# A message-passing layer: node rows laid in pairs on a partition, and two skipped loops put inside one

## The chip, the cores and the metric

The kernel runs on one core of a Trainium2 chip. The metric is the time on the device in microseconds, lower is better. Before the change it is 2068.9 us, the median of 3 runs (2066.65 to 2071.43).

## What is computed

A graph layer over 6250 nodes with 128 features and 200,000 edges, sorted by destination. Cut to what matters, with `ssp(z) = softplus(z) - log 2`:

```python
h = jnp.maximum(layernorm(x), 0.0)
xw = h @ W_in                                       # [6250, 128]
W = ssp(edge_attr @ W_f1 + b_f1) @ W_f2 + b_f2      # [200000, 128], edge_attr has 20 columns
x_ij = xw[dst] * (W * edge_weight)
out = segment_sum(x_ij, src, num_segments=6250)
result = x + ssp(out @ W_o1 + b_o1) @ W_o2 + b_o2
```

The gather goes by `dst`, which is sorted, and the sum by `src`, which is random.

## The kernel before

The nodes are padded to 6272, that is 49 tiles of 128, and the edges to 784 chunks of 128. Four chunks (512 edges) are a quad; there are 391 quads, and one step of the main loop belongs to each. All of it is one function, `tile_gnn`, with many helpers. Up to line 1254 the order of the work on every engine is written out by hand (`tc.manual_schedule()`): the loop at line 1208 runs its fixed calls for step `i`, and between them the hooks that `at(i, point, fn, ...)` has put there. SyncE (SP) issues nearly all DMAs, in program order on one queue; a DMA waits there until the one that used its semaphore eight DMAs earlier has landed.

**Nodes.** `groups` are pairs of node tiles (256 nodes; the last has one). For each, `xt_load` (L175 to 177) brings rows of `x` to `x_sb`, `prep_stat` to `prep_x3` (L181 to 255) make the layer norm, relu and the product with `W_in`, split in three bfloat16 parts, and `tab_write` (L257) writes them to a table `tab` in DRAM, three rows a node. Group 0 comes before the loop, the others at intervals of nine steps within it.

**Edges.** `load_sc` (L288) brings per 1024 edges the edge features, the relative destinations and, for each 256 edges, a window of 21 nodes of `tab`. PE makes the filter (L313, L494, L505) and picks the nodes' rows (L497), ACT scales (L510), DVE multiplies (L520). The sum by source goes two ways. Part of the quads are scattered by indirect DMAs that POOL issues (`scatter`, L579 to 583) and that add into four accumulators in DRAM, `accs[0]` to `accs[3]`, of [6400, 128] float32 each, with further rows behind them for a list. The others are sorted and summed on PE (L687, L781) and added into `accT` (L792), an SBUF tile of [128 features, 6272 nodes].

**Accumulator 0.** It takes no scatters after a certain point (`RET`). From then on `r0_load` (L1062) brings it in groups of 512 nodes (`tgroups`: 12 of four tiles, one of a single tile), `r0_tp` (L1068) transposes the tiles on PE, and `r0_add` (L1075) adds them into `accT`.

**The flags.** At the end of the loop a few operations (L1256 to 1270) find whether an edge fell outside its window, a slot was full, or a value was large. Two loops over register trip counts follow: `For_i(0, anew)` at L1273 zeroes the accumulators, and `For_i(0, trips)` at L1280 does all edges anew, chunk by chunk. With the given inputs both run no trip. In front of each, every engine loads the trip count (L1272, L1278), and going past a loop, each engine passes a chain of waits on the semaphores of all DMAs and engines.

**The tail** (L1349 to 1446) is also ordered by hand. For each group of 512 nodes `t_load` (L1353) brings three accumulators from DRAM, three loads of 256 KB; POOL adds two of them (`t_sum1`, L1359), POOL or DVE the third (`t_sum2`, L1364); PE transposes (`t_tp`, L1370), DVE adds `accT` (`t_cp`, L1376), PE multiplies by `W_o1` (`t_z`), ACT makes the softplus in three passes (`t_ln`), DVE completes it (`t_act`), PE multiplies by `W_o2` (`t_y`), and `t_out` (L1412) adds `x_sb` (with the bias already in it) and writes the result. Five groups are loaded ahead. At step `j` SP issues the loads of group `j + 5` first and then the output of group `j - 4`, so three outputs stand between the last loads:

```python
for j in range(-1, TG + 4):
    if TAIL_AHEAD <= j + TAIL_AHEAD < TG:
        for k in (1, 2, 3):
            t_load(j + TAIL_AHEAD, k)
    ...
    if 0 <= j - 4 < TG:
        t_out(j - 4)
```

In `x`, the accumulators, `accT` and the result, partition `p` of tile `t` holds node `128 t + p`: a partition's piece of one tile is one row of 128 float32, 512 bytes in one run in DRAM. In the table a piece is 768 bytes.

Of the kernel before, what the change touches and what calls it, by code (L numbers as in the profile page):

```python
# [20 lines left out]
P = 128  # L21
# [33 lines left out]
def tile_gnn(ctx: ExitStack, tc: tile.TileContext, x, fB, cT, srcT, srcr, dstr, win_, wf1, wf2, bias, bo1c, wo1,  # L55
# [780 lines left out]
    with tc.manual_schedule():  # L836
# [238 lines left out]
        def r0_add(g):  # L1075
            o, T = tgroups[g]
            v = accT[:, o:o + T * P]
            u = pst["p", g].rearrange("p t f -> p (t f)")[:, :T * P]
            nc.vector.tensor_tensor(v, u, v, op=ALU.add)
# [188 lines left out]
    flagi = cp.tile([1, 2], I32, name="flagi")  # L1268
# [3 lines left out]
    anew = nc.values_load(flagi[:, 1:2], min_val=0, max_val=1, skip_runtime_bounds_check_because="0 or 1")  # L1272
    with tc.For_i(0, anew, 1):  # L1273
        nc.vector.memset(accT, 0.0)
        for k in range(1, NACC):
            for j in range(ZR):
                zero_piece(nc.sync, k, j)
    trips = nc.values_load(flagi[:, 0:1], min_val=0, max_val=NCH,  # L1278
                           skip_runtime_bounds_check_because="0 or the number of chunks")
    with tc.For_i(0, trips, 1) as ci:  # L1280
        dcol = wk.tile([P, 1], I32, bufs=1, tag="dcol", name="dcol")
        nc.sync.dma_start(dcol, dstr.rearrange("s (e o) -> (s e) o", o=1)[bass.ds(ci * P, P), :])
        rcol = wk.tile([P, 1], BF16, bufs=1, tag="rcol", name="rcol")
        nc.sync.dma_start(rcol, reld.rearrange("s (e o) -> (s e) o", o=1)[bass.ds(ci * P, P), :])
        scol = wk.tile([P, 1], I32, bufs=1, tag="scol", name="scol")
        nc.sync.dma_start(scol, srcr.rearrange("s (e o) -> (s e) o", o=1)[bass.ds(ci * P, P), :])
        ccol = wk.tile([P, 1], F32, bufs=1, tag="ccol", name="ccol")
        nc.sync.dma_start(ccol, cT[:, bass.ds(ci, 1)])
        xcol = wk.tile([P, 1], BF16, bufs=1, tag="xcol", name="xcol")
        cm = wk.tile([1, 1], I32, bufs=1, tag="cm", name="cm")  # L1290
        nc.sync.dma_start(cm, cmap[0:1, bass.ds(ci, 1)])
        _, (cr,) = nc.values_load_multi_w_load_instructions(
            cm, engines=[SP], min_val=0, max_val=EP // P - 1,
            skip_runtime_bounds_check_because="a column of the table")
        nc.sync.dma_start(xcol, dropd[:, bass.ds(cr, 1)])
        sb = wk.tile([P, P], I32, bufs=1, tag="oeq", name="fsb")
        nc.sync.dma_start(sb, srcr.rearrange("s e -> (s e)")[bass.ds(ci * P, P)].unsqueeze(0).to_broadcast([P, P]))
        ft = wk.tile([P, P], BF16, tag="oh", name="fft")
        nc.vector.memset(ft[96:P, :], 1.0)
        fsel = fsd.rearrange("b g (r e) -> b (g r) e", r=RB)  # L1300
        for g, m in FPARTS:
            nc.sync.dma_start(ft[g * RB:(g + m) * RB, :], fsel[bass.ds(ci // (BE // P), 1), :m * RB,
                                                               bass.ds((ci % (BE // P)) * P, P)]
                              .rearrange("o m e -> (o m) e"))
        x3 = wk.tile([P, 3, P], BF16, tag="pt", name="fx3")
        nc.gpsimd.indirect_dma_start(out=x3.rearrange("p k f -> p (k f)"), out_offset=None,
                                     in_=tab.rearrange("(n k) f -> n (k f)", k=3),
                                     in_offset=bass.IndirectOffsetOnAxis(ap=dcol[:, 0:1], axis=0))
        ok = wk.tile([P, 4], F32, bufs=1, tag="ok", name="ok")
        nc.vector.tensor_scalar(ok[:, 0:1], rcol, float(WIN), None, op0=ALU.is_ge)  # L1310
        nc.vector.tensor_scalar(ok[:, 1:2], rcol, 0.0, None, op0=ALU.is_lt)
        nc.vector.tensor_tensor(ok[:, 2:3], ok[:, 0:1], ok[:, 1:2], op=ALU.add)
        nc.vector.tensor_tensor(ok[:, 2:3], ok[:, 2:3], zcol[:, 3:4], op=ALU.max)
        nc.vector.scalar_tensor_tensor(ok[:, 3:4], ok[:, 2:3], xcol, ccol, op0=ALU.max, op1=ALU.mult)
        xw = wk.tile([P, P], F32, bufs=1, tag="rm", name="fxw")
        nc.vector.tensor_tensor(xw, x3[:, 0], x3[:, 1], op=ALU.add)
        nc.vector.tensor_tensor(xw, xw, x3[:, 2], op=ALU.add)
        z = ps.tile([P, P], F32, tag="A", name="fz", bufs=4)
        nc.tensor.matmul(z, ws, ft[:K1, :], start=True, stop=True)
        e = wk.tile([P, P], F32, tag="a", name="fe")  # L1320
        nc.scalar.activation(e, z, AF.Abs)
        nc.scalar.activation(e, e, AF.Exp, scale=-1.0)
        nc.scalar.activation(e, e, AF.Ln, bias=half, scale=0.5)
        a = wk.tile([P, P], F32, tag="a", name="fa")
        nc.vector.scalar_tensor_tensor(a, z, 0.0, e, op0=ALU.max, op1=ALU.add)
        W = ps.tile([P, P], F32, tag="A", name="fW", bufs=4)
        nc.tensor.matmul(W, onesb[HB:], b2rep[HB:, 0, :], start=True, stop=False)
        nc.tensor.matmul(W, a, w2, start=False, stop=True)
        m = wk.tile([P, 132], F32, tag="xc", name="fm")
        nc.vector.tensor_copy(m[:, 128:129], wgt)  # L1330
        nc.vector.scalar_tensor_tensor(m[:, :P], W, ok[:, 3:4], xw, op0=ALU.mult, op1=ALU.mult)
        eq = wk.tile([P, P], F32, tag="eq", name="feq", bufs=3)
        nc.vector.tensor_tensor(eq, sb, scol.to_broadcast([P, P]), op=ALU.is_equal)
        pp = ps.tile([P, 132], F32, tag="B", name="fpp", bufs=4)
        nc.tensor.matmul(pp[:, :129], eq, m[:, :129], start=True, stop=True)
        s = wk.tile([P, P], F32, bufs=1, tag="dg", name="fs")
        nc.scalar.copy(s, pp[:, :P])
        dlt = wk.tile([P, 2], F32, bufs=1, tag="dlt", name="dlt")
        nc.vector.tensor_scalar(dlt[:, 0:1], scol, trash, None, op0=ALU.subtract)
# [256 lines left out]
```

## Time and profile before

| | |
|---|---|
| median of 3 runs | 2068.9 us (2066.65 to 2071.43) |
| the profiled execution | 2079.2 us, its span 2077.4 us |
| PE's mean granted clock | 0.963 |
| busy share of PE, DVE, ACT, POOL | 90%, 80%, 71%, 79% |
| DMA packets, bytes | 381188, 272.57 MB, mean 131 GB/s |

PE is TensorE's matrix products and PEld its weight loads, DVE is VectorE, ACT ScalarE, POOL GpSimd, SP SyncE; a q behind a name (SPq) is the engine's instruction queue, where waits, branches and DMA issues stand. A group of instructions is shown as line, engine, operation, result<-operands, count, then busy time, mean duration in ns, and the idle time ahead of it with what ended it. A row of the view by time has the start in us, the duration, the engine, the line and the count. A row of the view by stretches has the stretch, its length, the busy time and the instructions of PE, PEld, DVE, ACT and POOL, then PE's granted clock (1.00 is full), the mean busy share of the 16 DMA engines (above 1 where packets overlap), and the rate in GB/s. A row of the view of one source line has the durations (min/median/max, ns) and the first and last start.

### The profile page before, as it was taken

To read this page: it belongs to the slowest core of one execution; us is meant where nothing else is said; L and a number is where in the kernel's file an instruction comes from. 1 tells how busy PE (TensorE), PEld (TensorE's weight loads), DVE (VectorE), ACT (ScalarE), POOL (GpSimd) and SP (SyncE) were. 2 spreads that over 40 slices of the span, in tenths; PEclk is the share of its full clock that TensorE was granted. 3 is DMA by queue.
4 is the path that set the end of the run, shared out by engine and by line. 5 is a ranking of instruction groups with operands and counts; after the bars stand their busy time and mean duration, and the time that the engine had idled before them with its cause. 6 is when DMAs were issued, how large, how long until landed. Compare 5 with 4: busy or idle time off the path is not lost. (4 is left out here: it accounts for less than half of the span.)

```text
span 2077.4 us, 57578 instructions
## 1 busy us (share of the span) xinstructions
PE 1862.5 (90%) x20381; PEld 1288.0 (62%) x20381; DVE 1659.4 (80%) x4448; ACT 1482.8 (71%) x4083; POOL 1643.9 (79%) x1040
## 2 busy tenths in 40 slices
PE   3579988899999999999999999999999999999956
PEld 2456666566666666666666666666666666677734
DVE  3678887797888888988988978979889788787635
ACT  2468776777776777777678777777877777788714
POOL 3578787888877888887878878888888888888774
PEclk9679999999999999999999999999999999999977
DMA  7887766667766766766667666676676676667648
GB/s 238 227 210 147 125 118 120 121 112 130 130 118 114 126 127 119 139 123 123 120 120 130 120 119 118 118 124 117 120 134 108 124 121 111 110 119 131 130 48 239
DMA packets 381188, 272.57 MB, mean 131 GB/s; under 512 B 97727, under 2 KB 341354, under 8 KB 380898
## 3 DMA queue, kind: packets, MB, share of 16 engines
q0 software_dynamic: 143728, 71.30, 35.2%
q1 hardware_dynamic: 236882, 197.50, 34.1%
q8 instruction: 161, 2.64, 0.5%
q14 instruction: 129, 1.06, 0.2%
q10 hardware_dynamic: 288, 0.07, 0.0%
HBM read 154.45 MB, written 114.24 MB: 129 GB/s over the span
## 5 line engine op out<-in xcount | busy, mean ns | idle before, releaser
L582 POOL DMA_INDIRECT acc<-s,lji x768 | 1245.7, 1622 | 266.6 <-issue 180.3
L687 PE MATMUL pq<-pt,pm 128*128 128x387 bf16 x2688 | 533.0, 341 | 44.6 <-DVE pt L676 10.6
L510 ACT ACTIVATE xc<-xg,cb 128x128 f32<-128x128 f32 x1564 | 446.4, 371 | 135.7 <-PE xg L497 119.9
L505 PE MATMUL W<-w,a 128*128 128x128 f32 x3128 | 464.1, 292 | 0.1
L505 PEld LDWEIGHTS W<-w,a 128*128 128x128 f32 x3128 | 388.4, 195 | 42.3 <-issue 3.1
L687 PEld LDWEIGHTS <-pm 128*128 128x128 bf16 x2688 | 260.3, 99 | 233.4 <-issue 37.2
L693 ACT CAST mst<-pq 128x387 bf16<-128x387 f32 x672 | 302.2, 481 | 135.0 <-PE pq L687 96.5
L781 PE MATMUL un<-so,mst 32*128 32x392 bf16 x8064 | 374.5, 327 | 17.3 <-DVE pr L627 7.0
L781 PEld LDWEIGHTS <-mst 32*128 32x128 bf16 x8064 | 227.8, 93 | 157.1 <-issue 60.2
L323 ACT ACTIVATE a<-a,con 128x512 f32<-128x512 f32 x391 | 282.3, 722 | 12.7
L582 POOL DMA_INDIRECT acc<-s,ji x123 | 200.2, 1628 | 80.4 <-issue 26.4
L318 ACT ACTIVATE a<-z 128x512 f32<-128x512 f32 x391 | 238.3, 610 | 26.8 <-PE z L313 17.2
L676 DVE TENSOR_TENSOR pt<-pt 128x512 f32<-128x512 f32 x336 | 231.8, 690 | 5.8
L662 DVE TENSOR_SCALAR pm<-iot,pos 128x576 bf16<-128x576 f16 x672 | 221.8, 391 | 0.0
L792 DVE TENSOR_TENSOR accT<-un,accT 128x392 f32<-128x392 f32 x320 | 158.6, 558 | 73.7 <-PE un L781 37.5
L520 DVE TENSOR_TENSOR s<-W,xc 128x512 f32<-128x512 f32 x192 | 131.9, 687 | 85.9 <-ACT xc L510 52.0
L766 DVE TENSOR_SCALAR so<-iot,mst 128x392 bf16<-128x392 f16 x672 | 191.0, 344 | 6.7 <-PE un L781 6.7
L582 POOL DMA_INDIRECT acc<-os,oji x96 | 156.4, 1629 | 31.2 <-issue 18.0
L497 PE MATMUL xg<-wn,oh 63*128 63x128 bf16 x1564 | 157.3, 222 | 15.8 <-ACT xc L510 9.4
L313 PE MATMUL z<-ft,ws 123*128 123x512 bf16 x391 | 152.0, 389 | 15.7 <-DVE iotl L941 9.4
L494 PE MATMUL W<-b2rep,onesb 64*128 64x512 bf16 x391 | 153.9, 394 | 0.0
L520 DVE TENSOR_TENSOR pt<-W,xc 128x512 f32<-128x512 f32 x168 | 115.2, 686 | 47.9 <-ACT xc L510 29.5
(209 smaller groups left out, 2435.5 us busy)
## 6 DMA issues: line engine op xcount, KB each, us to landing
rb<-reld SPq DMA_DIRECT2D x391, 64.0 KB
fsd<-f SPq DMA_DIRECT2D x49, 480.0 KB
ft<-fsd SPq DMA_DIRECT2D x195, 120.0 KB
sb<-src SPq DMA_DIRECT2D x169, 128.0 KB
fb<-in_fB_dram SPq DMA_DIRECT2D x49, 320.0 KB
ft<-fsd SPq DMA_DIRECT2D x195, 80.0 KB
wn<-tab SPq DMA_DIRECT2D x782, 15.8 KB
acc<-s,lji POOLq DMA_INDIRECT x768
```

Of the source, the lines that this page charges most:

```text
L318: nc.scalar.activation(a, st[q]["z"], AF.Exp)
L323: nc.scalar.activation(a, a, AF.Ln, bias=half, scale=0.5)
L505: nc.tensor.matmul(W[:, c, :], st[q]["a"][:, c * P:(c + 1) * P], w2, start=False, stop=(c == 3))
L510: nc.scalar.mul(xc[:, c, :], st[q]["xg"][:, c, :], late["c", q // CQ][:, 4 * (q % CQ) + c:4 * (q % CQ) + c + 1])
L520: nc.vector.tensor_tensor(m[:, :, :P], st[q]["W"], st[q]["xc"], op=ALU.mult)
L582: nc.gpsimd.indirect_dma_start(out=accs[k][:rows, :], out_offset=bass.IndirectOffsetOnAxis(ap=ji, axis=0), in_=s, in_offset=None, compute_ ...
L662: nc.vector.tensor_scalar(pm[:, c], iot[:, :SLOTS], rk[r]["pos"][:, 4 * j + c:4 * j + c + 1], None, op0=ALU.is_equal)
L676: nc.vector.tensor_tensor(pt[:, :, k * P:(k + 1) * P], a, high(a), op=ALU.subtract)
L687: nc.tensor.matmul(t[:, :PW], mp[q]["pm"][:, c, s * P:(s + 1) * P], high(mp[q]["pt"][:, c:c + 1, :PW])[:, 0], start=(c == 0), stop=(c == 3))
L693: nc.scalar.copy(mp[q]["ms", s][:, :PW], mp[q].pop(("q", s))[:, :PW])
L766: nc.vector.tensor_scalar(so, iotw[:, :GN], w[:, 3 * P // 2:3 * P // 2 + 1], None, op0=ALU.is_equal)
L781: nc.tensor.matmul(ts[g][:, :GN], mp[q]["ms", s][v, k * P:(k + 1) * P], mp[q]["oh"][v], start=(q == qs[0] and k == 0), stop=(q == qs[-1] a ...
```

## The change

Two things are changed.

The first is the layout of nodes. Within 256 nodes, partition `p` holds nodes `2p` and `2p + 1` in its two tiles, in place of `p` and `p + 128`. Four helpers say so: `rows` for a DRAM tensor, `wide` for a row-major SBUF tile, `nodes` for columns of `accT`, `tiles` for a transposed tile. The loads of `x`, of accumulator 0 and of the tail's three accumulators and the writes of the result then move runs of 1024 bytes, the table's writes runs of 1536. `accT` keeps its columns in the order of the nodes, so `r0_add` and `t_cp` reach it at every second column. Single tiles (the last of each grouping) stay as they were.

The second is the flags: `flagi` gets a third element, 0 or 1, and the two loops with the loads of their trip counts stand inside an outer loop over it. The bodies are the same, moved in by four columns.

On the engines, nothing changes its place up to the flags. Behind them DVE has one operation more, and every engine has one more loop head and loop end, of which the walk past it runs; the two inner ones are inside the part that is passed. GpSimd's wait and increment for the indirect DMAs (before, at the second loop) now stand at the outer loop too.

```diff
+    def rows(t, o, T):
+        n = min(T, 2)
+        return t[o:o + T * P, :].rearrange("(h p t) f -> p h (t f)", p=P, t=n)
+
+    def wide(t, T):
+        return t.rearrange("p (h t) f -> p h (t f)", t=min(T, 2))
+
+    def nodes(t, o, T):
+        return t[:, o:o + T * P].rearrange("f (h p t) -> f h t p", p=P, t=min(T, 2))
+
+    def tiles(t, T):
+        return t[:, :T].rearrange("f (h t) p -> f h t p", t=min(T, 2))
+
     def xt_load(g):
         o, T = groups[g]
-        nc.sync.dma_start(x_sb[:, o // P:o // P + T], x[o:o + T * P, :].rearrange("(t p) f -> p t f", p=P))
+        nc.sync.dma_start(wide(x_sb[:, o // P:o // P + T], T), rows(x, o, T))
...
     def tab_write(g):
         o, T = groups[g]
-        nc.sync.dma_start(tab[o * 3:(o + T * P) * 3, :].rearrange("(t p k) f -> p t k f", t=T, k=3),
+        nc.sync.dma_start(tab[o * 3:(o + T * P) * 3, :].rearrange("(p t k) f -> p t k f", t=T, k=3),
                           pst[g]["x3"][:, :T])
...
         def r0_load(g):
-            nc.sync.dma_start(t_[:, :T], accs[0][o:o + T * P, :].rearrange("(t p) f -> p t f", p=P))
+            nc.sync.dma_start(wide(t_[:, :T], T), rows(accs[0], o, T))
...
         def r0_add(g):
             o, T = tgroups[g]
-            v = accT[:, o:o + T * P]
-            u = pst["p", g].rearrange("p t f -> p (t f)")[:, :T * P]
-            nc.vector.tensor_tensor(v, u, v, op=ALU.add)
+            v = nodes(accT, o, T)
+            nc.vector.tensor_tensor(v, tiles(pst["p", g], T), v, op=ALU.add)
...
-    flagi = cp.tile([1, 2], I32, name="flagi")
+    flagi = cp.tile([1, 3], I32, name="flagi")
+    nc.vector.tensor_scalar(flagi[:, 2:3], flag1, 0.0, None, op0=ALU.is_gt)
...
-    anew = nc.values_load(flagi[:, 1:2], min_val=0, max_val=1, skip_runtime_bounds_check_because="0 or 1")
-    with tc.For_i(0, anew, 1):
...
-    trips = nc.values_load(flagi[:, 0:1], min_val=0, max_val=NCH,
-                           skip_runtime_bounds_check_because="0 or the number of chunks")
-    with tc.For_i(0, trips, 1) as ci:
...
+    redo = nc.values_load(flagi[:, 2:3], min_val=0, max_val=1, skip_runtime_bounds_check_because="0 or 1")
+    with tc.For_i(0, redo, 1):
+        anew = nc.values_load(flagi[:, 1:2], min_val=0, max_val=1, skip_runtime_bounds_check_because="0 or 1")
+        with tc.For_i(0, anew, 1):
...
+        trips = nc.values_load(flagi[:, 0:1], min_val=0, max_val=NCH,
+                               skip_runtime_bounds_check_because="0 or the number of chunks")
+        with tc.For_i(0, trips, 1) as ci:
...
         def t_load(g, k):
-            nc.sync.dma_start(t_[:, :T], accs[k][o:o + T * P, :].rearrange("(t p) f -> p t f", p=P))
+            nc.sync.dma_start(wide(t_[:, :T], T), rows(accs[k], o, T))
...
         def t_cp(g):
-            o, w = tgroups[g][0], tgroups[g][1] * P
-            oT = tk.tile([P, 512], F32, tag="oT", name="oT")
-            nc.vector.tensor_tensor(oT[:, :w], tl[g]["tp"].rearrange("p t f -> p (t f)")[:, :w], accT[:, o:o + w],
-                                    op=ALU.add)
-            tl[g]["oT"] = oT
+            o, T = tgroups[g]
+            oT = tk.tile([P, 4, P], F32, tag="oT", name="oT")
+            nc.vector.tensor_tensor(tiles(oT, T), tiles(tl[g]["tp"], T), nodes(accT, o, T), op=ALU.add)
+            tl[g]["oT"] = oT.rearrange("p t f -> p (t f)")
...
-            full = min(T, max(0, (N - o) // P))
-            if full:
-                nc.sync.dma_start(out[o:o + full * P, :].rearrange("(t p) f -> p t f", p=P), y[:, :full])
-            rest = min(N - o, w) - full * P
-            if rest > 0:
-                nc.sync.dma_start(out[o + full * P:o + full * P + rest, :], y[:rest, full, :])
+            if N - o >= w:
+                nc.sync.dma_start(rows(out, o, T), wide(y[:, :T], T))
+            else:
...
```

More of the change, by code (lines that the diff above doesn't have):

```diff
@@ L1273, in tile_gnn @@
[L1273 to L1278, printed above, removed]
-                           skip_runtime_bounds_check_because="0 or the number of chunks")
[L1280 to L1339, printed above, removed]
-        nc.vector.scalar_tensor_tensor(dlt[:, 1:2], pp[:, 128:129], wgt2, dlt[:, 0:1], op0=ALU.is_lt, op1=ALU.mult)
-        ji = wk.tile([P, 1], I32, bufs=1, tag="fji", name="fji")
-        nc.vector.tensor_scalar(ji, dlt[:, 1:2], trash, None, op0=ALU.add)
-        nc.gpsimd.indirect_dma_start(out=accs[1][:, :], out_offset=bass.IndirectOffsetOnAxis(ap=ji[:, 0:1], axis=0),
-                                     in_=s, in_offset=None, compute_op=ALU.add)
@@ L1416, in t_out @@
             nc.vector.tensor_tensor(y[:, :T], tl[g]["y"][:, :T], x_sb[:, o // P:o // P + T, :], op=ALU.add)
-            full = min(T, max(0, (N - o) // P))
-            if full:
-                nc.sync.dma_start(out[o:o + full * P, :].rearrange("(t p) f -> p t f", p=P), y[:, :full])
-            rest = min(N - o, w) - full * P
-            if rest > 0:
-                nc.sync.dma_start(out[o + full * P:o + full * P + rest, :], y[:rest, full, :])
+            if N - o >= w:
+                nc.sync.dma_start(rows(out, o, T), wide(y[:, :T], T))
+            else:
+                n = min(T, 2)
+                for h in range(T // n):
+                    b = o + h * n * P
+                    full, rest = divmod(min(max(N - b, 0), n * P), n)
+                    if full:
+                        nc.sync.dma_start(out[b:b + full * n, :].rearrange("(p t) f -> p t f", t=n),
+                                          y[:full, h * n:(h + 1) * n])
+                    if rest:
+                        nc.sync.dma_start(out[b + full * n:b + full * n + rest, :].rearrange("(p t) f -> p t f", p=1),
+                                          y[full:full + 1, h * n:h * n + rest])
             del tl[g]
```

68 lines of the change are left out of this document (added).

## Prediction

> **What bounds the kernel now.** The page's first section was read first, then the busy times by stretches of the span, then the order of time on POOL and on SP's queue near the end.
>
> ```profile
> span 2077.4 us, 57578 instructions
> PE 1862.5 (90%) x20381; PEld 1288.0 (62%) x20381; DVE 1659.4 (80%) x4448; ACT 1482.8 (71%) x4083; POOL 1643.9 (79%) x1040
> ```
>
> ```profile
> 31.00:40.00 9.00, 4.56 (x21) 3.80 (x22) 4.50 (x6) 1.32 (x2) 2.69 (x5) 1.00 1.03 416
> 52.00:55.00 3.00, 1.43 (x12) 1.04 (x11) 1.87 (x6) 0.71 (x4) 0.00 (x0) 1.00 0.98 378
> 200.00:1800.00 1600.00, 1503.53 (x17062) 1029.99 (x17055) 1351.28 (x3668) 1206.56 (x3334) 1318.71 (x813) 0.99 0.69 121
> 2000.00:2018.00 18.00, 7.18 (x99) 4.12 (x97) 5.04 (x18) 0.00 (x0) 14.39 (x10) 0.68 0.40 36
> 2024.00:2036.00 12.00, 4.05 (x11) 2.08 (x12) 1.29 (x2) 0.57 (x1) 6.37 (x6) 0.50 1.13 292
> 2036.00:2048.00 12.00, 10.41 (x40) 6.82 (x41) 6.95 (x11) 7.43 (x12) 7.92 (x7) 0.66 1.15 291
> 2048.00:2058.00 10.00, 8.55 (x55) 6.43 (x53) 7.71 (x13) 7.46 (x12) 6.57 (x6) 1.00 1.12 309
> 2060.00:2076.00 16.00, 9.31 (x60) 7.12 (x58) 10.85 (x19) 8.30 (x14) 1.92 (x3) 0.96 0.43 132
> ```
>
> The columns after the length are PE, PEld, DVE, ACT and POOL, then PE's granted clock, the DMA engines' share and GB/s. Three stages show. In the edge loop (200 to 1800) PE is busy 1503.53 of 1600 us and the DMA engines 0.69: PE paces it. From 1960 on POOL takes over, one scatter after the other:
>
> ```profile
> 1984.12 1.54 POOL L582 DMA_INDIRECT acc<-s,ji  x1 [0.31 <-issue]
> ...
> 2015.60 1.54 POOL L582 DMA_INDIRECT acc<-os,oji  x1 [0.30 <-issue]
> ```
>
> Between these two POOL never idles more than 0.31 us: (2015.60 − 1984.12) / 17 = 1.85 us a scatter, while PE is busy 7.18 of 18 us. The last stage, the tail, begins with the loads of the accumulators on SP's queue:
>
> ```profile
> 2022.52 25.71 SPq L1356 DMA_DIRECT2D ta_in<-acc  x30
> 2048.34 0.78 SPq L1419 DMA_DIRECT2D out_dram<-yo  x1
> ...
> 2055.87 1.65 SPq L1356 DMA_DIRECT2D ta_in<-acc  x3
> 2057.61 15.41 SPq L1419 DMA_DIRECT2D out_dram<-yo  x9
> ```
>
> ```profile
> ta_in<-acc SPq DMA_DIRECT2D x36, 256.0 KB
> ...
> tab<-x SPq DMA_DIRECT2D x24, 192.0 KB
> x_sb<-in_x_dram SPq DMA_DIRECT2D x24, 128.0 KB
> ...
> r0t<-acc SPq DMA_DIRECT2D x12, 256.0 KB
> out_dram<-yo SPq DMA_DIRECT2D x12, 256.0 KB
> ```
>
> From 2022.52 to 2055.87 + 1.65 = 2057.52, so for 35.0 us, the DMA engines' share is above 1 and the rate stands near 300 GB/s: transfers pace this part. In it go 36 loads of 256 KB, 3 of 64 KB and 3 outputs of 256 KB, 10.42 MB, or 298 GB/s over all of it. After 2060 the share is 0.43: there the remaining groups run through DVE, ACT and PE, some 2 us each.
>
> **The change, part by part.**
>
> *The two loops.* Both run no trip here, and what they cost is the walk past them:
>
> ```profile
> L1273 SPq EVENT_SEMAPHORE  x20: 17/28/57, 2011.0 to 2019.5; - x20
> ```
>
> ```profile
> L1278 SPq TENSOR_LOAD <-flagi x1: 278/278/278, 2019.8 to 2019.8; - x1
> ```
>
> ```profile
> L1280 SPq COMPARE_BRANCH  x3: 33/33/39, 2020.2 to 2022.4; - x3
> ...
> L1280 POOLq INC_SWDGE_SEM  x1: 1160/1160/1160, 2020.6 to 2020.6; - x1
> ```
>
> SP reads the second trip count at 2019.8 only after the first loop's last wait at 2019.5, which stands on the last scatter of 2015.60 having landed. So the first walk is hidden under POOL's scatters and their landing, and the second, 2022.52 − 2019.8 = 2.7 us, is on the path. After the change one outer loop takes the place of both, with one such walk. Its new DVE operation (like L1269 below, 0.14 us, done by 2010.4) and its flag load lie under the scatters, with nine us of cover to 2019.5. What moves onto the one walk is POOL's 1.16 us increment. Behind it on POOL wait that engine's own last semaphores, and SP waits for POOL. POOL's last scatter ends at 2017.14 and the walk ended at 2019.5 in any case, so 1.16 us fit. If they stand behind the landing instead, up to 1.2 us come back. I take 0.2, nearest to the gap that is there: **−2.5 us**, bounds −2.7 and −1.5.
>
> *Packets of the tail.* Loads and outputs move 512-byte rows now, 1024 after (two neighbouring nodes). The last group (3 loads and the 53 KB output) keeps 512. What a 1024-byte packet costs no row shows alone, so it is bounded. At 291.5 GB/s over 16 engines a 512-byte packet takes 16 × 512 / 291.5 = 28.1 ns. From 31 to 40 us the bulk is POOL's zeroing, 2560 bytes to a row, at 416 GB/s: 16 × 2560 / 416 = 98.5 ns. On the line through both, 1024 bytes take 45.7 ns, 358 GB/s. From 52 to 55 us SP moves rows of 2560 and 2048 bytes (some 2300 on average) at 378 GB/s: 97 ns, and the line gives 48 ns, 342 GB/s. I take 47 ns, 349 GB/s. Ends: 298 (no gain) and 358. The 10.22 MB that change then need 29.3 us in place of 34.3: **−5.0 us**, bounds 0 and −5.7.
>
> Whether the engines can follow such a stream is asked of these rows of the tail:
>
> ```profile
> L1362 POOL TENSOR_TENSOR ta_in<-ta_in 128x512 f32<-128x512 f32 x12 | 15.2, 1268 | 20.1 <-DMA ta_in<-acc 18.3 <-DVE oT L1379 1.5
> ...
> L1402 DVE SCALAR_TENSOR_TENSOR ta<-tz,nbo,tl 128x512 f32<-128x512 f32 x12 | 8.9, 744 | 1.0 <-ACT tl L1396 1.0
> L1396 ACT ACTIVATE tl<-te,con 128x512 f32<-128x512 f32 x12 | 8.7, 722 | 0.4
> L1393 ACT ACTIVATE te<-tz,bo_sb 128x512 f32<-128x512 f32 x12 | 8.2, 685 | 51.7 <-DMA ta_in<-acc 42.9 <-PE tz L1386 8.5
> L1416 DVE TENSOR_TENSOR yo<-ty,x_sb 128x512 f32<-128x512 f32 x12 | 8.2, 685 | 3.0 <-DMA out_dram<-yo 2.0 <-PE tz L1386 0.5 <-PE ty L1409 0.5
> L1379 DVE TENSOR_TENSOR oT<-tp,accT 128x512 f32<-128x512 f32 x12 | 8.1, 683 | 0.0
> ...
> L1394 ACT ACTIVATE te<-te 128x512 f32<-128x512 f32 x12 | 7.6, 631 | 0.4
> ...
> L1368 DVE TENSOR_TENSOR ta_in<-ta_in 128x512 f32<-128x512 f32 x6 | 4.2, 692 | 30.3 <-POOL ta_in L1362 30.3
> ```
>
> POOL waits 18.3 us for loads. A group costs POOL 1.27 or 2.54 us (1.9 on average), ACT 0.69 + 0.63 + 0.72 = 2.04, DVE 0.68 + 0.74 + 0.69 and in every other group 0.69 more, 2.45 (their starts lie closer, some 0.6 us apart). Three loads at 349 GB/s take 2.25 us, and with an output 3.0. So transfers still end last, but by little. What is late next is the run-out after the last load, which I leave as long as it is: its outputs go out singly at a DMA share of 0.43, and the last of them keeps its packets (0 to −0.2, taken 0).
>
> *Strided adds.* `t_cp` and `r0_add` read or write `accT` at every second column now, 8 bytes apart.
>
> ```profile
> L1379 DVE TENSOR_TENSOR oT<-tp,accT 128x128 f32<-128x128 f32 x1 | 0.3, 281 | 0.0
> ```
>
> ```profile
> L676 DVE TENSOR_TENSOR pt<-pt x336: 674/693/755, 110.2 to 1951.8; 128x512 f32<-128x512 f32 x168
> ```
>
> ```profile
> 2009.82 0.29 DVE L1079 TENSOR_TENSOR accT<-rtp,accT 128x128 f32<-128x128 f32 x1
> ...
> 2010.28 0.14 DVE L1269 TENSOR_SCALAR flagi<-flag 1x1 int32<-1x1 f32 x1
> ...
> 2032.43 0.68 DVE L1379 TENSOR_TENSOR oT<-tp,accT 128x512 f32<-128x512 f32 x1
> ...
> 2071.42 0.89 DVE L1416 TENSOR_TENSOR yo<-ty,x_sb 128x512 f32<-128x512 f32 x2 [0.46 <-PE ty L1409]
> ```
>
> No row shows this step. The nearest is L676, which reads one operand as every second bf16 and takes 693 ns, as the plain L1379 does with 683. From above: if each of the four inner runs cost as much as the instruction of 128 columns, 4 × 281 = 1.12 us, +0.44 an operation. I take 0, as in L676; a gain is excluded, since as many elements pass. At +0.44 the 12 `t_cp` add 5.3 us to DVE, most of it inside DVE's idle time while loads pace; in the last four groups 4 × 0.44 = +1.8 us show. The 13 `r0_add` (L1079, the last at 2009.82) lie under POOL's scatters, which end at 2017.14; that cover gone, the last ones would add 0.44 each.
>
> *Node loads, table writes, r0 loads.* 24 loads of 128 KB, 24 writes of 192 KB and 12 of the r0 loads get rows twice as long. They lie in the loop that PE or POOL paces, at a DMA share of 0.4 to 0.7. A node load needs 0.45 us of 16 engines now (256 × 28.1 / 16) and 0.38 after. Taken 0. If the cover were gone, 24 × 0.07 and as much for the writes would be gained, −3 us. SP's queue keeps its order, nothing is moved past anything, and no instruction is added in the loop.
>
> *Sum.* −2.5 − 5.0 = −7.5 us. The profiled execution took 2079.2 us (span 2077.4), 10.3 more than the median of the three runs. The tail's terms are differences within it and carry over: 2079.2 becomes 2071.7, and the median 2068.9 becomes **2061.4 us**.
>
> **The rivals.**
>
> *A: the packet's size gains nothing.* Either DMA goes on at 512 bytes, or 292 GB/s is a limit on reading and not on packets. For it: the rate is flat at 292 and 291 while the share is 1.13 and 1.15, so packets overlap and still gain nothing. Against: 309 with outputs mixed in, and 378 and 416 with longer rows. Only the loops are gained: 2068.9 − 2.5 = 2066.4 us, 0.12%. The Trainium skill, page "DMA: Bandwidth & Descriptors", its table at the top, speaks for this one: it puts the smallest transfer at line rate at 512 bytes, so that 1024 would bring nothing. By that, the −5.0 is 0; the rates quoted above, 292 against 378 and 416, do not agree with it.
>
> *B: the engines take the bound.* PE's clock is 0.50 and 0.66 in the first two stretches of the tail, and from 2036 to 2048 PE is busy 10.41 of 12 us. A mean of 0.66 is 0.5 for eight of the twelve us and 1.0 for four, so the clock is up at about 2044. If PE cannot follow until then, only the loads from there to 2057.5 are gained; of their time 5.0 / 34.3 = 0.146 goes, and 13.5 × 0.146 = 2.0 us. 2068.9 − 2.5 − 2.0 = 2064.4 us. For it: the 10.41. Against: POOL, ahead of PE in each group, waited for loads, and the lost lead can be made up after 2044.
>
> *C: slower, by the strided adds.* The mechanism is `t_cp` on DVE taking several times as long. From the first `t_cp` to the last sum with x (2032.4 to 2072.3) there are 39.9 us, 34.9 after the gain, and DVE's rows of 512 columns above add up to 8.9 + 8.2 + 8.1 + 4.2 = 29.4 of them: 5.5 us are free. The gain of 7.5 is eaten when 12 × p − 5.5 = 7.5, so from p = 1.08 us more an operation, which then takes 1.76 us. At three times its time (p = 1.37) the sum is 2061.4 + 16.4 − 5.5 = 2072.3 us. Against it: L676. The Trainium skill, page "SBUF — State Buffer", in its note on SBUF cachelines, has lines of 16 bytes that need two hits each for full rate; a step of 8 bytes gives two, and by that rule this rival does not happen. No run here shows it.
>
> **How the numbers follow.** The forecast has 0.72, B 0.13, A 0.11, C 0.04. About 0.2%, or 4.1 us, is what a measurement of this kernel tells from no change; the three runs lie from 2066.65 to 2071.43, so ±2.4. Faster is below 2064.8: nearly all of the forecast (0.68), half of B (0.07), a little of A (0.03), 0.78. Slower is C and a stray, 0.05; the same, 0.17. The range starts at the forecast with the best packet and the full walk (−8.4, 2060.5) less 2.4, 2058, and reaches over B to just past A, 2067. Outside are C, some of A and the forecast's own tails, about 0.15.
>
> **What would show it.** In the profile after, the walk past the loops on SP ends some 0.2 us after its last wait on the scatters, and the first load of `ta_in` is issued near 2019.9 (if the loop's length is the same). The 30 first loads take about 21.9 us on SP's queue in place of 25.71, at some 349 GB/s; 292 there means A. A rate that falls while POOL no longer waits for loads and PE is busy at a clock of 0.5 means B. `oT<-tp,accT` stays at 0.68 us; from 1.76 us on it is C. What would make the whole wrong is a shift of more than 4 us in the loop before 1985, which none of the steps here produces.

## The result, and the profile after

The changed kernel takes 2056.39 us, the median of 11 runs (2050.39 to 2058.33), where the kernel before took 2063.74 beside it (11 runs, 2059.13 to 2071.43). The ratio is 0.9954, with a 95% interval from 0.9937 to 0.9970, so −9.5 us, between −13.0 and −6.2. By the medians it is −7.35 us. The forecast of the change, −7.5, lies inside that interval. The time itself, 2056.39, lies below the range, which began at 2058. The three runs of before on which the prediction stood (median 2068.9) are among those 11; the other eight have a median of 2062.3. In the last set of runs below, one run of the changed kernel took 3492.9 us and is left out of its ratio.

The profiled execution took 2051.26 us. Its page begins so:

```profile
span 2049.5 us, 57496 instructions
...
PE 1855.4 (91%) x20381; PEld 1284.7 (63%) x20381; DVE 1658.4 (81%) x4449; ACT 1491.2 (73%) x4083; POOL 1636.9 (80%) x1040
```

The busy times are those of before within 0.6%, and the span is 27.9 us shorter. So most of what the two profiles differ by is idle time, and far more of it went than was forecast. These lines show where. The last scatter on POOL, in the view of POOL by time:

```profile
1994.96 1.54 POOL L595 DMA_INDIRECT acc<-os,oji  x1 [0.30 <-issue]
```

And the tail's loads and outputs on SP's queue, by time:

```profile
1999.02 21.77 SPq L1371 DMA_DIRECT2D ta_in<-acc  x30
2021.73 0.38 SPq L1432 DMA_DIRECT2D out_dram<-yo  x1
...
2027.75 1.70 SPq L1371 DMA_DIRECT2D ta_in<-acc  x3
2029.85 15.44 SPq L1432 DMA_DIRECT2D out_dram<-yo  x9
```

From these rows the end of the program splits in three. The walk, from the start of the last scatter to the first load: 1999.02 − 1994.96 = 4.06 us, before 2022.52 − 2015.60 = 6.92. The loads, to the end of the last issue: 2029.45 − 1999.02 = 30.4, before 35.0. The run-out, from there to the end of the span: 20.05, before 19.88. Together 54.5 us in place of 61.8, so −7.3. The other 20.6 us lie ahead of the last scatter (1994.96 against 2015.60), in the loop, where the forecast puts nothing of the change on the path; the experiments come back to them.

What released the first load, in the view of the outer loop's line:

```profile
L1286 SPq EVENT_SEMAPHORE  x21: 17/28/28, 1988.0 to 1998.8; - x21
...
L1286 POOLq INC_SWDGE_SEM  x1: 1160/1160/1160, 1994.0 to 1994.0; - x1
```

The last wait starts at 1998.8 and the first load at 1999.02: 0.2 us after it, as forecast. POOL's increment of 1.16 us ran at 1994.0, ahead of the last scatter.

The tail by stretches (columns as in the prediction):

```profile
2000.00:2006.00 6.00, 0.00 (x0) 0.00 (x0) 0.00 (x0) 0.00 (x0) 0.78 (x1) 0.50 0.88 250
2006.00:2012.00 6.00, 3.29 (x10) 1.96 (x10) 1.29 (x2) 0.00 (x0) 4.20 (x4) 0.50 1.01 335
2012.00:2024.00 12.00, 9.33 (x41) 6.04 (x41) 7.16 (x12) 7.75 (x12) 10.09 (x9) 0.80 1.10 349
2024.00:2030.00 6.00, 6.00 (x43) 4.80 (x42) 6.00 (x10) 5.59 (x9) 4.54 (x4) 1.00 1.09 375
```

Where before ran at 291 GB/s, this runs at 349, the rate that was estimated from 47 ns a packet. The first six us are slow in both (250 here; 253 GB/s in before's first 9.5 us). In the last stretch PE and DVE are busy all 6.00 us: the engines have hardly any room left there.

Two groups of the tail, by line and shape:

```profile
L1377 POOL TENSOR_TENSOR ta_in<-ta_in 128x512 f32<-128x512 f32 x12 | 15.3, 1275 | 13.6 <-DMA ta_in<-acc 13.5
...
L1394 DVE TENSOR_TENSOR oT<-tp,accT 128x512 f32<-128x512 f32 x12 | 8.1, 685 | 0.0
```

`t_cp` with its strided read of `accT` takes 685 ns, before 683. POOL's idle time ahead of its additions fell from 20.1 to 13.6 us, nearly all of it now for loads.

### The profile page after: what moved, and what is told of

It is laid out like the page before. It is cut to its first block, busy times and chain, and to the rows that moved or that the text cites. A ratio compares the mean times of both kernels' runs of the same rounds, so it can differ in the third digit from the quotient of the medians.

```text
span 2049.5 us, 57496 instructions
## 1 busy us (share of the span) xinstructions
PE 1855.4 (91%) x20381; PEld 1284.7 (63%) x20381; DVE 1658.4 (81%) x4449; ACT 1491.2 (73%) x4083; POOL 1636.9 (80%) x1040
## 5 line engine op out<-in xcount | busy, mean ns | idle before, releaser
L595 POOL DMA_INDIRECT acc<-s,ji x123 | 196.0, 1594 | 78.7 <-issue 26.5
```

The lines of the kernel that those rows point to most:

```text
L595: nc.gpsimd.indirect_dma_start(out=accs[k][:rows, :], out_offset=bass.IndirectOffsetOnAxis(ap=ji, axis=0), in_=s, in_offset=None, compute_ ...
```

## The experiments

The theory (T): the walk past the second loop and the packets of the tail's loads make the whole gain, and the loop gives nothing. Its rival (R): part of the gain comes from the main loop, from node loads, table writes or the r0 loads, since the profiled loop got 20.6 us shorter. A second pair of questions came with the result: whether size is really what the packets gain by, and what ends last now.

Each set of runs was made on one chip with the kernel before beside it. The rows shown are from the view of the accumulators by tile: the tail's loads and the last scatter, durations min/median/max in ns, then the first and the last start. The table at the end gives the three parts of all kernels.

**The loops alone.** Kernel before with only the flags part of the diff (outer loop over `redo`, the third element of `flagi`).

> The kernel before with the two skipped loops inside one, and the old layout. Theory T (the gain is the walk past one loop plus the tail's transfers, and the main loop gives nothing): 2.5 to 2.9 us less than before; from the issue of the last scatter to the first load of the tail about 4.1 us, as after (1994.96 to 1999.02), in place of 6.9; the tail from first load to the end of the span 55 us, as before. Rival R (the longer node rows also gain in the main loop, which would make the measured gain of 9.5 us larger than the tail's 7.3): the same for this run. If the walk's saving were only the clock of the profiled runs, no change.

```profile
L1359 SPq DMA_DIRECT2D ta_in<-acc x39: 359/808/1260, 2021.5 to 2056.2; - x39
L582 POOL DMA_INDIRECT acc<-os,oji x1: 1543/1543/1543, 2017.5 to 2017.5; - x1
```

The walk is 4.06 us, the loads 35.05, as T says. The ratio is 0.9990 [0.9974, 1.0006], −2.1 us, which fits −2.5 and does not exclude nothing. The gain of 2.8 us is read from the trace, and only half confirmed by the times.

**The tail's loads alone.** Kernel before with its two loops; `t_load` in pairs, and `t_cp` puts the nodes back in order by writing `oT` at every second column.

```diff
-            nc.sync.dma_start(t_[:, :T], accs[k][o:o + T * P, :].rearrange("(t p) f -> p t f", p=P))
+            nc.sync.dma_start(wide(t_[:, :T], T), rows(accs[k], o, T))
...
+            nc.vector.tensor_tensor(nodes(oT, 0, T), tiles(tl[g]["tp"], T), nodes(accT, o, T), op=ALU.add)
```

> The kernel before with only the tail's three accumulator loads in pairs (1024 bytes a packet); the sums with accT are written back in node order, so x, the table, the r0 loads and the results keep 512 and 768 bytes, and both skipped loops stay. Theory T: the 30 first loads at some 345 GB/s, the tail from first load to the end 4 us shorter (about 51 us), the time 3.5 to 4.5 us less than before. Rival R: the same 4 us, and the rest of the layout's gain is missing, 2 to 4 us against the whole change less the loops.

```profile
L1369 SPq DMA_DIRECT2D ta_in<-acc x39: 320/360/897, 2017.5 to 2047.0; - x39
L595 POOL DMA_INDIRECT acc<-os,oji x1: 1543/1543/1543, 2010.7 to 2010.7; - x1
```

The walk is back at 6.84 us, the loads last 29.8 in place of 35.0, and the ratio is 0.9981 [0.9966, 0.9996], −3.9 us.

**All the rest.** Layout of the changed kernel everywhere but in the tail's loads; the two loops as before; `t_cp` reads PSUM at every second column.

> The kernel before with the pair layout everywhere but in the tail's accumulator loads: x, the table, the r0 loads and the results move 1024 and 1536 bytes, the accumulator loads 512; the adds of accT reach PSUM and accT at every second column; both skipped loops stay. Theory T: 0 to 0.6 us less than before (three outputs between the loads), the tail 54 to 55 us. If every second column of PSUM costs DVE time, oT shows it, and the tail is that much longer. Rival R: 2 to 5 us less than before, from the main loop.

```profile
L1368 SPq DMA_DIRECT2D ta_in<-acc x39: 375/767/2382, 2016.5 to 2050.7; - x39
L595 POOL DMA_INDIRECT acc<-os,oji x1: 1543/1543/1543, 2009.7 to 2009.7; - x1
```

Ratio 1.0000 [0.9984, 1.0015]: node loads, table writes, r0 loads, outputs and strided adds together show no gain. The interval is wide, from −3.3 to +3.1 us: R, which put 2 to 5 us here, falls but for its low end. That leaves the 20.6 us of the profiled loop to something that is not the change.

**The changed kernel again**, in the same set.

> The changed kernel once more, on the chip of the three parts. Theory T: the sum of the parts, 7 to 8 us less than before, the tail 50 to 51 us from first load to end; the place of the last scatter differs from run to run by some us whichever kernel it is. Rival R: 9 to 12 us less, more than the first two parts add up to.

```profile
L1371 SPq DMA_DIRECT2D ta_in<-acc x39: 319/360/1152, 2018.9 to 2047.8; - x39
L595 POOL DMA_INDIRECT acc<-os,oji x1: 1543/1543/1543, 2014.9 to 2014.9; - x1
```

Ratio 0.9967 [0.9952, 0.9982], −6.8 us; the parts above add up to −2.1 − 3.9 − 0 = −6.0. The tail is as fast as in the first profile, but the last scatter starts at 2014.9 and not at 1995.0. The same program had a loop 20 us longer. The median moved with it: 2065.52 us here, against 2072.25 for the kernel before (35 runs).

**Four rows a packet.** The changed kernel, with four neighbouring nodes on a partition for the tail's loads, so 2048 bytes. `x_sb` and the output stay in pairs, and `t_cp` becomes two operations of 256 columns, which read `accT` every 16 bytes.

```diff
+            n = min(T, 4)
+            nc.sync.dma_start(t_[:, :T].rearrange("p (h t) f -> p h (t f)", t=n),
+                              accs[k][o:o + T * P, :].rearrange("(h p t) f -> p h (t f)", p=P, t=n))
...
+                u = oT.rearrange("f (h b) (q a) -> f a h b q", b=2, a=2)
+                v = tl[g]["tp"].rearrange("f (a b) (h q) -> f a h b q", b=2, h=2)
+                w = accT[:, o:o + 4 * P].rearrange("f (h q a b) -> f a h b q", h=2, a=2, b=2)
+                for a in range(2):
+                    nc.vector.tensor_tensor(u[:, a], v[:, a], w[:, a], op=ALU.add)
```

> The changed kernel, with four neighbouring nodes on a partition for the tail's 36 loads of 256 KB: packets of 2048 bytes in place of 1024 (t_cp in two halves, about 0.16 us more an operation on DVE). Theory S, the size of the packets paces the tail and transfers still end last: on the line through 28.1 ns (512 bytes, 291.5 GB/s) and 47.1 ns (1024 bytes, 348 GB/s) a 2048-byte packet takes 85 ns, 385 GB/s; 9.44 MB need 24.5 us in place of 27.1, so the loads last about 27 us from the first issue to the end of the last and the kernel is 2.6 us faster than the changed one in the same runs. Rival E, the engines (PE at its low clock, or POOL) now end last: the loads last 29 to 30 us as in the changed kernel, POOL waits for loads much less than 13.5 us, and the time is within 1 us of the changed kernel's.

By stretches:

```profile
2017.00:2035.00 18.00, 11.09 (x36) 6.30 (x36) 8.64 (x14) 5.91 (x9) 15.07 (x12) 0.58 1.04 379
...
2043.00:2053.00 10.00, 8.56 (x53) 6.44 (x53) 10.00 (x17) 7.18 (x12) 3.29 (x4) 1.00 0.40 136
```

By line and shape:

```profile
L1403 DVE TENSOR_TENSOR oT<-tp,accT 128x256 f32<-128x256 f32 x24 | 13.7, 617 | 0.0
```

The rate rose as S says, to 379 GB/s (385 forecast). The kernel did not get faster than the changed one but slower: 2062.59 us, ratio 0.9989 [0.9974, 1.0003], and the changed kernel beside it (below) had 2056.76. So S fails on the time, and E, which put it within 1 us of the changed kernel's, is out by 5.8 us as well. What E has right is that an engine ends last, but it is another than the ones it named: POOL's wait for loads went only from 13.5 to 11.6 us, and DVE is busy 10.00 of 10 us, since 256 columns take 617 ns where the 512 of the changed kernel take 685. I had put 0.16 us more on an operation; it was 2 × 617 − 685 = 549 ns, 6.6 us over twelve groups. The loads last 30.6 us and the run-out is 23.25 in place of 20: the last nine loads stand on SP's queue behind the first outputs, and the first output went out 3.5 us after the last of the 30 first loads, in place of 0.9 to 1.0.

**Four rows, packets cut at 512.** The same, with `ta_in` of 132 columns a node, so that the rows in DRAM still lie together but no packet is over 512 bytes.

```diff
-            t_ = la.tile([P, 4, P], F32, tag=f"a{k}", name="ta_in")
+            t_ = la.tile([P, 4, 132], F32, tag=f"a{k}", name="ta_in")
...
+            nc.sync.dma_start(t_[:, :T, :P], accs[k][o:o + T * P, :].rearrange("(p t) f -> p t f", t=n))
```

> As the one with four rows, in the same order of nodes, but the tile in SBUF has 132 columns a node in place of 128, so each packet ends at 512 bytes while the rows read from HBM still lie next to each other. Theory S (size of a packet): the loads go back to about 292 GB/s, last about 35 us, and the kernel is some 7 us slower than with four rows and 4.6 us slower than the changed kernel. Rival O (what counts is that neighbouring rows are read together, in whatever packets): the loads last as with four rows, 27 to 30 us, and the time is within 1 us of that kernel's.

```profile
2014.00:2030.00 16.00, 13.42 (x53) 8.50 (x54) 10.97 (x19) 8.70 (x13) 11.41 (x9) 0.75 1.13 294
```

294 GB/s, and the loads last 34.6 us: the size of the packet sets the rate, not that neighbouring rows are read together (in the trace's packet records, the packets here have 512 bytes). O falls. The time, 2061.35 us (ratio 0.9984 [0.9970, 0.9997]), is 4.6 above the changed kernel's, as S said, but level with four rows and not 7 us slower: the slower `t_cp`, which cost that kernel its gain, shows less beside the longer loads (run-out 20.7 in place of 23.3).

**No loop at all.** The changed kernel without lines 1285 to the end of the outer loop (the fallback is left out).

> The changed kernel without the skipped loops (the fallback, which runs no trip on these inputs, is left out, so part of the computation for other inputs is missing). Theory H, the one walk that is left lies under the landing of the last scatter: the first load is still issued about 4.0 us after the last scatter, and the time is within 0.5 us of the changed kernel's. Rival W, the walk that is left still costs what the second one cost: first load 1.3 to 2.8 us after the last scatter, 1.2 to 2.7 us faster than the changed kernel.

SP's first three loads by time, and the last scatter from the view by tile:

```profile
1999.96 0.36 SPq L1296 DMA_DIRECT2D ta_in<-acc  x1
...
2001.84 0.36 SPq L1296 DMA_DIRECT2D ta_in<-acc  x1
...
2003.65 0.36 SPq L1296 DMA_DIRECT2D ta_in<-acc  x1
```

```profile
L595 POOL DMA_INDIRECT acc<-os,oji x1: 1542/1542/1542, 2000.3 to 2000.3; - x1
```

2057.00 us, ratio 0.9963 [0.9948, 0.9978], beside 2056.76 for the changed kernel: the walk that is left costs nothing that shows in the times, though their intervals, some 3 us either way, would hide the 1.2 to 2.7 us of rival W. H is wrong on the moment of the first load. It goes out before the last scatter, 4.4 us earlier than with the walk (4.15 us after it in the changed kernel beside this one). But the three loads of the first group come 1.8 to 1.9 us apart, the third 3.4 us after the last scatter, and only from there on do the rest follow; the loads last 32.5 us and the sum from the last scatter to the end is 53.1 against 54.2. SP's waits from 1996 to 2034 us (who waited, for whom, then us in total, times and the longest) show what held these three, namely scatters that had not landed, the last of all among them:

```profile
SPq L1296 <- DMA acc<-s,ji: 24.3, 2, 22.8
...
SPq L1296 <- DMA acc<-os,oji: 1.4, 1, 1.4
```

So without the walk the landing of the scatters holds these loads. What the earlier start still won was waited away: after the 30 first loads SP's queue stood still for 2.3 us ahead of the first output, where the changed kernel's stands for 0.9 to 1.0.

**The changed kernel a third time**, beside the three above.

> The changed kernel as it is, beside the others. Theory T (walk and tail transfers, nothing in the loop): 5 to 9 us faster than the kernel before in the same runs, ratio 0.9957 to 0.9976; in its profile 4.0 us from the last scatter to the first load and 29 to 31 us of loads. On the level of both: if it moves from one set of runs to another whatever the kernel, the median of the kernel before lies anywhere from 2060 to 2075 and the changed kernel's follows it; rival, 2068.9 was a stray of three runs: before lies at 2063.7 +- 1.5 again.

```profile
L1371 SPq DMA_DIRECT2D ta_in<-acc x39: 319/360/1341, 2008.0 to 2037.6; - x39
L595 POOL DMA_INDIRECT acc<-os,oji x1: 1542/1542/1542, 2003.9 to 2003.9; - x1
```

2056.76 us against 2065.00 (31 runs), ratio 0.9960 [0.9942, 0.9978]. The level was lower than in the set before, for both kernels; 2065.00 by itself would also fit the rival's 2063.7 ± 1.5, but 2072.25 ahead of it and 2078.43 behind it do not.

**Four rows, order restored by PE.** Loads of 2048 bytes; the transposes write every fourth column of PSUM, so `t_cp` is one operation again and reads 8 bytes apart.

```diff
+            v = tp.rearrange("f t p -> f (t p)")[:, :T * P].rearrange("f (p t) -> f t p", t=T)
             for t in range(T):
-                nc.tensor.transpose(tp[:, t, :], tl[g][1][:, t, :], idt)
+                nc.tensor.transpose(v[:, t, :], tl[g][1][:, t, :], idt)
```

> Four rows a packet (2048 bytes) as in the first kernel with four rows, but t_cp stays one operation of 512 columns: the 49 transposes write every fourth column of PSUM, so that the nodes lie in order there, and t_cp reads PSUM and accT 8 bytes apart as the changed kernel reads accT. Theory V, the first kernel with four rows lost on DVE alone (two t_cp of 617 ns a group in place of one of 684, DVE busy 10.00 of 10.00 us): t_cp is back at about 685 ns, the transposes stay at 309 ns on average, the loads last 27 to 29 us and the kernel is 0.5 to 2.6 us faster than the changed kernel in the same runs. Rival P, a strided write of PSUM slows the transposes: above 450 ns each, up to 49 x 0.3 = 15 us more on PE of which the ones after the clock is up show, 2 to 8 us slower than the changed kernel. Rival E2, no engine is slower and the time is still that of the changed kernel within 0.5 us: then the run-out and the start of the tail end last, not the loads.

By line and shape:

```profile
L1392 PE MATMUL tp<-idt,ta_in 128*128 128x128 f32 x49 | 9.0, 311 | 21.7 <-DMA ta_in<-acc 20.8 <-DVE ta_in L1385 0.8
...
L1398 DVE TENSOR_TENSOR oT<-tp,accT 128x512 f32<-128x512 f32 x12 | 8.0, 678 | 0.0
```

By stretches:

```profile
2020.00:2036.00 16.00, 9.13 (x36) 5.57 (x36) 6.84 (x10) 6.00 (x9) 14.76 (x12) 0.73 1.02 370
...
2043.00:2053.00 10.00, 10.00 (x65) 7.65 (x64) 10.00 (x16) 8.85 (x14) 4.03 (x5) 1.00 0.54 184
```

SP's queue by time, and its waits from 2010 to 2045 us:

```profile
2014.23 19.36 SPq L1372 DMA_DIRECT2D ta_in<-acc  x30
2036.63 0.39 SPq L1437 DMA_DIRECT2D out_dram<-yo  x1
```

```profile
SPq L1437 <- DVE yo L1435: 2.6, 1, 2.6
```

`t_cp` is back at 678 ns, the strided write of PSUM costs nothing (311 ns; P falls), and the loads run at 370 GB/s. Yet they last 28.8 us and the run-out 20.9, 53.9 from the last scatter to the end, where the changed kernel had 53.3 to 54.5. SP's queue shows why: after the 30 first loads it stood still for 3.0 us, because DVE had not yet made the first output, and the last nine loads stand behind that. In the kernel before, this gap is 0.1 us, in the changed kernel 0.9 to 1.0. PE and DVE are busy 10.00 of 10 us once the clock is up. So the traces speak for E2: above 1024 bytes the engines end last, and faster loads only wait. The times, 2066.41 us and a ratio of 0.9945 [0.9923, 0.9966], can't be told from the changed kernel's (below); by themselves they would allow V's gain of 0.5 to 2.6 us too.

**`t_cp` in halves at 8 bytes.** The changed kernel with two operations of 256 columns in the same three inner dims (2, 2 and 64) as with four rows, but `accT` read every 8 bytes.

> The changed kernel with t_cp in two halves of 256 columns, with three inner dims of 2, 2 and 64 as in the kernel with four rows, but accT is read 8 bytes apart in place of 16. Theory L, a step of 16 bytes is what made 256 columns take 617 ns: on the line through 281 ns (128 columns) and 684 ns (512) a half takes 415 ns here, t_cp 0.83 us a group, and the kernel is 0 to 1.5 us slower than the changed one. Rival D, the short runs of 64 (or the third dim) make it: about 617 ns a half here too, DVE busy nearly all of the run-out, and the kernel 4 to 6 us slower than the changed one.

```profile
L1401 DVE TENSOR_TENSOR oT<-tp,accT 128x256 f32<-128x256 f32 x24 | 8.9, 416 | 0.0
```

416 ns against 415 worked out, so the short runs cost nothing, and D falls. What is left for the 617 ns is the step of 16 bytes in reading `accT` (that kernel also wrote `oT` 8 bytes apart, which took 683 ns for 512 columns with the tail's loads alone). The Trainium skill, page "SBUF — State Buffer", in its note on SBUF cachelines, says that a line of 16 bytes needs two hits for full rate: two here at 8 bytes and no loss, one at 16 bytes and 617 / 416 = 1.5 times as long. The trace agrees with it on both. The time is 2066.20 us, ratio 0.9934 [0.9915, 0.9954], not slower than the changed kernel.

**The changed kernel a fourth time**, in that set.

> The changed kernel as it is, to compare with. Theory T: ratio to the kernel before 0.9957 to 0.9976 again, 4.0 us from the last scatter to the first load, 29 to 31 us of loads. On the level: if it belongs to the chip or the set of runs (2072.25 and 2065.0 so far, 35 and 31 runs), the kernel before may have any median from 2060 to 2075 here and the changed one lies 5 to 9 us below it; rival, the level is one and both medians were strays of their sets: then 2068.5 +- 2 for before and 2061.5 +- 2 for this.

```profile
L1371 SPq DMA_DIRECT2D ta_in<-acc x39: 320/360/1544, 2024.7 to 2053.5; - x39
L595 POOL DMA_INDIRECT acc<-os,oji x1: 1543/1543/1543, 2020.6 to 2020.6; - x1
```

2069.48 us against 2078.43 for the kernel before (12 runs), ratio 0.9949 [0.9929, 0.9968]. The ratio is a little below the 0.9957 to 0.9976 that were expected, whose greater part lies inside the interval. The rival on the level, one level around 2068.5 and the rest strays, falls.

The parts, from the rows of SP's queue and POOL by time and each span (us):

| kernel | last scatter | walk | loads | run-out | last scatter to end |
|---|---|---|---|---|---|
| before | 2015.60 | 6.92 | 35.0 | 19.9 | 61.8 |
| loops alone | 2017.48 | 4.06 | 35.0 | 19.4 | 58.5 |
| tail's loads alone | 2010.71 | 6.84 | 29.8 | 20.3 | 57.0 |
| the rest | 2009.72 | 6.80 | 34.6 | 19.7 | 61.1 |
| changed, four times | 1994.96, 2014.92, 2003.87, 2020.56 | 4.06, 4.02, 4.15, 4.09 | 30.4, 29.2, 29.9, 29.2 | 20.1, 20.3, 20.2, 20.1 | 54.5, 53.5, 54.2, 53.3 |
| four rows | 2008.32 | 4.14 | 30.6 | 23.3 | 58.0 |
| four rows, 512 | 1998.52 | 4.22 | 34.6 | 20.7 | 59.5 |
| no loop | 2000.26 | −0.30 | 32.5 | 21.0 | 53.1 |
| four rows, PE | 2010.02 | 4.21 | 28.8 | 20.9 | 53.9 |
| halves | 2010.12 | 4.10 | 29.4 | 20.0 | 53.6 |

None of these is shown to beat the changed kernel.

## Why the prediction was right or wrong, point by point

*The two loops, −2.5 us: right.* The walk went from 6.92 to between 4.02 and 4.15, so −2.8; without the change it is 6.80 to 6.92 in all three profiles. The 0.2 us kept back for POOL's increment was not needed, as the increment runs ahead of the last scatter. Most of the walk that remains lies under the landing of the last scatter, but not all of it: in the trace's records of SP (first profile of the changed kernel) the wait for that landing ends at 1998.17, and further waits of the chain fill the 0.85 us to the first load. The kernel without the walk is not faster by any amount that shows.

*Packets of the tail, −5.0 us: right.* The loads went from 35.0 to 29.2 to 30.4, mean 29.7, so −5.3; the steady rate is 349 GB/s, the one estimated. One of the two stretches behind the 47 ns was misread, without harm: in the trace's packet records POOL's zeroing (90% of the bytes from 31 to 40 us) has packets of 5120 bytes, 196 ns in the median, each with two rows of 2560. On the line through these 1024 bytes take 46.9 ns and not 45.7, so the better end of the bounds, 358 GB/s, falls to 349. And the records of before held the packet itself: from 200 to 1800 us the 1024-byte packets of the hardware queue took 46 ns in the median. Padding to 512 bytes with the rows side by side brought it back to 294. Rival A, and the rule at the top of the page "DMA: Bandwidth & Descriptors" of the Trainium skill that 512 bytes are enough for line rate, do not hold here: 294, 349 and 379 GB/s at 512, 1024 and 2048 bytes.

*Strided adds, 0: right.* 685 ns for 683. Rival C, a `t_cp` that costs more, did not come at 8 bytes; at 16 bytes it did, with its mechanism (DVE full in the run-out), though at +0.55 us and not at +1.37. C had counted 5.5 us of DVE's time as free; at 2048 bytes a packet, the 6.6 us more on DVE left the stretch from the last scatter to the end 3.5 to 4.7 us longer than in the changed kernel, where C's sum gives 1.1.

*Node loads, table writes, r0 loads, 0: right as far as the runs tell.* 1.0000 [0.9984, 1.0015] for all of them together, which leaves room for 3 us.

*Rival B, engines take the bound: not at 1024 bytes, but next in line.* The run-out grew by 0.2 to 0.4 us, and at 2048 bytes nothing more was gained.

*The base: wrong, and this is the step that failed.* In the sum it reads "2079.2 becomes 2071.7, and the median 2068.9 becomes 2061.4"; in the range it was let go by ±2.4, the spread of three runs. Of the 5.0 us by which 2056.39 lies below 2061.4, this base makes 5.2 (2063.74 for 2068.9), and the change itself 0.15 the other way; that the change comes so close is luck, as its interval is 6.8 us wide. The level moves much more between sets of runs than within those three. Before had 2063.74 in the comparison (11 runs), then 2072.25 (35), 2065.00 (31) and 2078.43 (12); the changed kernel, beside it, had 2056.39, 2065.52, 2056.76 and 2069.48. The differences of the medians are −7.35, −6.7, −8.2 and −9.0 (by the ratios −9.5, −6.8, −8.3 and −10.6): the medians lie within 1.5 us of −7.5, while the level covers 14.7 us for before and 13.1 for the changed kernel. The forecast of 2061.4 lies within the changed kernel's levels, but up to 8.1 us from one of them (2069.48), which is more than the whole change.

*"What would make the whole wrong is a shift of more than 4 us in the loop before 1985, which none of the steps here produces."* The shift came, 20.6 us in the two profiles, and indeed no step produced it: the changed kernel's own last scatter starts anywhere from 1994.96 to 2020.56. The condition was the right one to name, but its price was not in the range.

What makes the loop's length vary is not settled. The last three sets came from three chips; whether it is the chip or the moment was not told apart. PE's granted clock does not make the difference between those sets: its median over the runs of before is 0.965, 0.966 and 0.9645 where the times are 2072.25, 2065.00 and 2078.43. Within each of these sets of before the times do fall with the clock, by 0.6 to 1.1 us for 0.001 on a straight line through the runs, but that makes at most 1.6 of the 13.4 us between the last two. One place in the traces can be named. At about 350 us ACT waits once for a scatter to land (view of ACT's waits from 340 to 380 us), in the first profile of the changed kernel:

```profile
ACT oji L768 <- DMA acc<-os,oji: 9.7, 1, 9.7
```

and in its second:

```profile
ACT oji L768 <- DMA acc<-os,oji: 14.9, 1, 14.9
```

The two loops differ by 20.0 us, and this one wait by 5.2. But it does not set the loop's length: in the third and fourth profiles it is 13.0 and 13.1 us, and their last scatters lie 16.7 us apart. The cause stays open.

## What to carry to other kernels

Predict the difference and the time apart: the difference comes from the trace, the level from several sets of runs, and where only one set of three is at hand the range must allow for a shift that no step of the change explains, here up to 0.7%. Two parts of a path that can be read off as intervals (here last scatter to first load, and first load to last) repeat within about 1.3 us from one execution to the next, even where the whole program does not, so judge a small change by them. When a transfer is made faster, look at once at the busy shares of the engines behind it: here 1024 bytes a packet took the slack that there was, and 2048 bought nothing that showed.

## What the runs showed of the hardware that was not expected

- A DVE operation that reads one float32 operand at a step of 16 bytes takes 617 ns for 256 columns, at 8 bytes 416 ns (the first also wrote its result 8 bytes apart).
- Packets of the hardware queue in the loop of before (200 to 1800 us, medians of the trace's packet records) took 27 ns at 512 bytes, 46 at 1024, 84 at 2048 and 102 at 2560.
- Transposes that write every fourth column of PSUM (311 ns on average) are no slower than those that write in a row (322 ns in the kernel with halves).
- The rate at 2048 bytes, 379 GB/s, lies near the line through the packet times of 512 and 1024 bytes (385 worked out).
- In the tail's first six us the transfers run at 250 GB/s in place of the later 349 (changed kernel, first profile), with PE, DVE and ACT still idle; the cause stays open.
- The same program's loop ends up to 25.6 us apart in four profiled executions (1994.96 to 2020.56).
